# Score matmuls of an attention, split from four tiles of 32 by 128 into eight tiles of 32 by 64

## The chip, the cores and the metric

The kernel runs on one core of a Trainium2 chip. The metric is the device time of one execution in microseconds (us); lower is better. A core has engines that run at the same time and wait for one another by semaphores: TensorE (PE: matrix products, with a weight load before each one), VectorE (DVE), ScalarE (ACT), GpSimd (POOL), and SyncE (SP), which issues the DMAs here. Matrix products write into PSUM, which has eight banks of 128 partitions by 512 float32; everything else lies in SBUF.

## What is computed

Four layers follow one another on 16 images of 384 channels and 16 by 16 pixels, seen as 2 groups (`b`) of 2048 tokens. All is float32.

- Layer 0, attention with 12 heads of 32 channels over 2048 tokens: `out = alpha*v + beta*softmax(q k^T / sqrt(32)) v - gamma*mean(v)`, where `v` is the input itself and `q`, `k` are a product of the input with `qk_w`.
- Layer 1, a ConvNeXt block: a depthwise 7 by 7 convolution, a layer norm over channels, a product to 1536 channels, GELU, a global response norm, a product back to 384, and a residual.
- Layer 2: two Sobel filters, a product that fuses them, a layer norm, GELU, a residual.
- Layer 3: a 1 by 1, a 3 by 3 depthwise and a 1 by 1 convolution, a linear attention with 8 heads, and an MLP of 1536 channels.

## The kernel before

A block is 512 tokens of one group (`BLK`); there are eight, four for each group, and each is an SBUF tile of 128 partitions by 3 by 512.

**Attention.** `attention` runs over 6 units (`u`: a group `b` and a set `g` of four heads, which fill 128 partitions), in each over 4 query blocks (`n`), and in each over 16 key tiles of 128 tokens (`t`): 384 iterations. One iteration has two parts on TensorE.

- `scores(n, t)`: four matmuls, one for each head `h`. The keys are the weights (32 rows by 128 columns: the head's channels by 128 key tokens) and the queries stream through (32 rows by 512). The four stand in the four row groups of the array and run at once, and each fills a PSUM bank. Two heads share a tile `st` of two banks. The pool `pst` holds three such tiles, and an iteration takes two. ScalarE then forms the exponentials, two instructions of 128 by 1024 from `st` to `e`.
- `weighted(n, t, es)`, called one iteration later: four matmuls `av` with 128 rows by 32 columns, which stand in the four column groups. The denominators are not a product in each iteration: VectorE first adds up `ADDS[n]` (2 to 16) of the `e` tiles into `s`, and `weights` then sends the sums through TensorE against a column of ones (`dn`). `finish` inverts them and writes the block of layer 0.

At `t == SLOT` (5) a pair of projections `p` of the next block or unit is put in. A float32 matmul is carried out as two passes, so the profile shows two MATMUL and two LDWEIGHTS for each `pe.matmul`.

**What fills VectorE meanwhile.** After each iteration `attention` calls `fill(t, added)`. It asks `pace(t)` for the length of the iteration on TensorE (`pe`) and for the time that VectorE is needed in it (`dve`), and puts operations of layer 1 into what is left: for the first two blocks (`l1_0_0` and `l1_0_1`, the `leads`) the 7 by 7 convolution, 48 VectorE instructions for each of 3 channel groups after a first one on ScalarE (tile `y`), and after it the layer norm, as far as it comes. `pace` is a few constants; the first is 2.066 us for an iteration without `dn` and `p`.

**After attention.** A planner (`Plan.all`) orders all other work as the program is built, from estimated lengths, the tiles that are free and a rank of each task, starting from where `fill` left each task. PE, ACT and DVE then execute exactly that order (`InOrder`), so an instruction that waits holds all that is queued behind it on its engine. Layer 1 of a block has these steps by the names in the profile: taps `y<-l,vec,y`; sums `s_l` over channels and a product with ones `su_l` for the mean; `y<-su_l,y`; squares on ScalarE, their sum `s_l`, a product `sv_l` for the variance; a reciprocal, `y<-y,s_l`, an affine step on ScalarE; the first MLP product `ph_l` (36 matmuls of 128 by 128 by 512 for a block), GELU into `hid_l`, the response norm by way of `gx_l` and `pg_l`, and the second product `po_l`.

All matmuls, activations and vector operations are recorded through one helper (line 96), so the profile gives line 96 for all of them, and the names of the tiles tell them apart. `a<-b,c` reads: `a` is written from `b` and `c`.

Of the kernel before, what the change touches and what calls it, by code (L numbers as in the profile page):

```python
# [15 lines left out]
P = 128  # L16
# [7 lines left out]
HD = 32  # L24
# [32 lines left out]
TB = BLK // P  # L57
# [136 lines left out]
def pace(t):  # L194


    n, i = divmod(t - 1, NQC)
    adds = ADDS[n]
    pe, dve = 2.066, 2.275 if t and i % adds else 0.0
    at = i - adds - 1  # L200
    parts = sum(j * adds // 4 == at % adds for j in range(4)) if at >= 0 else 0
    if parts:
        pe += 0.22 * parts
    elif i == 1 and n > 0:
        pe += 0.87
    else:
        pe += 0.09
    if n > 0:
        dve += {2: 0.88, 3: 0.88, 4: 0.88, 5: 0.88, 6: 0.6, 7: 0.66}.get(i, 0.0)
    return pe, dve  # L210
# [187 lines left out]
def attention(tc, X, xt, L0, block, small, col, cols, ones, load_qk, banks, fill, bound):  # L398
# [4 lines left out]
    pe, act, dve = (InOrder(tc, e) for e in (nc.tensor, nc.scalar, nc.vector))  # L403
    units = [(b, g) for b in range(NB) for g in range(NC)]
    with ExitStack() as actx:
# [9 lines left out]
        def bank2(name):  # L415
            return pst.tile([P, 2, BLK], F32, tag="st", name=name)
# [38 lines left out]
        def unit(u, made, gm):  # L455

            b, g = units[u]
            q, keys, v = made["q"], made["k"], made["v"]
            adds = ADDS[u * NBLK : (u + 1) * NBLK]
            acc, sums = {}, {}  # L460

            def scores(n, t):
                es = []
                for i in range(2):
                    es.append(ep.tile([P, 2, BLK], F32, tag="e", name=f"e_{u}_{n}_{t}_{i}"))
                sts = [bank2(f"st_{u}_{n}_{t}_{i}") for i in range(2)]
                for h in range(4):
                    rows = slice(HD * h, HD * (h + 1))
                    pe.matmul(
                        sts[h // 2][:, h % 2, :],  # L470
                        keys[t // TB][rows, ts(t % TB, P)],
                        q[n][rows, :],
                        start=True,
                        stop=True,
                    )
                for i in range(2):
                    act.activation(es[i], sts[i], AF.Exp, scale=HD**-0.5)
                return es
# [56 lines left out]
            def finish(n, va, xg):  # L535
# [23 lines left out]
                for i, f in [*enumerate(todo), (8, check)]:  # L559
                    due.setdefault((k + 1) * NQC + 2 + i, []).append(f)  # L560

            return scores, weighted

        means = [channel_means(dve, op, X, cols, b, act if b else None) for b in range(NB)]
# [41 lines left out]
def conv_seq_kernel(  # L606
# [874 lines left out]
    if fast:  # L1481
# [5 lines left out]
        def fill(t, added=0.0):  # L1487
# [7 lines left out]
            if t % NQC == 9 and t > NQC:  # L1495
                u, i = divmod(t // NQC - 1, NBLK)
                plan.mark(("l0", u // NC, i, u % NC))
            length, work = pace(t)
            free = length + added - work - lag
            for task in (*leads, conv):  # L1500
# [157 lines left out]
```

## Time and profile before

| | |
|---|---|
| time, median of 3 executions | 2676.41 us (2674.85 to 2677.70) |
| span of the profiled execution | 2676.1 us |
| attention, first score matmul to the first `ph_l` | 20.7 to 1050.9 us |
| PE busy | 2645.0 us, 99% of the span |
| DVE busy | 2011.5 us, 75% |
| ACT busy | 1554.4 us, 58% |
| granted TensorE clock, mean | 0.996 |

The page states no time of the profiled execution apart from its span, which is the time from its first to its last instruction; it lies within the three times measured without the profiler and 0.3 us below their median, so sums are made against the span. "Busy" is the union of the intervals in which an engine has an instruction under way. For TensorE these intervals overlap, and their ends are modelled: 99% says that something was always under way, not that the array did useful work all the time. The starts of matmuls are what can be relied on.

### The profile page before, as it was taken

To read this page: it belongs to the slowest core of one execution; us is meant where nothing else is said; L and a number is where in the kernel's file an instruction comes from. 1 tells how busy PE (TensorE), PEld (TensorE's weight loads), DVE (VectorE), ACT (ScalarE), POOL (GpSimd) and SP (SyncE) were. 2 spreads that over 40 slices of the span, in tenths; PEclk is the share of its full clock that TensorE was granted. 3 is DMA by queue.
4 is the path that set the end of the run, shared out by engine and by line. 5 is a ranking of instruction groups with operands and counts; after the bars stand their busy time and mean duration, and the time that the engine had idled before them with its cause. 6 is when DMAs were issued, how large, how long until landed. Compare 5 with 4: busy or idle time off the path is not lost. (4 is left out here: it accounts for less than half of the span.)

```text
span 2676.1 us, 32807 instructions
## 1 busy us (share of the span) xinstructions
PE 2645.0 (99%) x12997; PEld 1061.0 (40%) x12997; DVE 2011.5 (75%) x2588; ACT 1554.4 (58%) x2314; POOL 7.4 (0%) x54
## 2 busy tenths in 40 slices
PE   9999999999999999899999999999999999999999
PEld 2223333233323323345444444444444444454443
DVE  6999999999999889999999999999652202722300
ACT  6787778878787888564565335357443542625201
POOL 0000000000000000000000000000000000000000
PEclk9999999999999999999999999999999999999999
DMA  3000000000000003000001001011001110000000
GB/s 150 5 13 1 9 9 5 13 1 5 13 1 1 1 13 113 18 1 0 1 1 48 24 12 33 27 36 36 24 24 36 48 36 24 0 1 1 12 17 20
DMA packets 29283, 55.69 MB, mean 21 GB/s; under 512 B 1728, under 2 KB 14400, under 8 KB 29120
## 3 DMA queue, kind: packets, MB, share of 16 engines
q1 hardware_dynamic: 29120, 53.51, 6.1%
q8 instruction: 104, 1.70, 0.3%
q14 instruction: 59, 0.48, 0.1%
HBM read 47.21 MB, written 6.29 MB: 20 GB/s over the span
## 5 line engine op out<-in xcount | busy, mean ns | idle before, releaser
L96 ACT ACTIVATE e<-st 128x1024 f32<-128x1024 f32 x768 | 742.4, 1024 | 89.2 <-PE st L96 81.3
L96 DVE SCALAR_TENSOR_TENSOR y<-l,vec,y 128x420 f32<-128x420 f32 (+8 forms) x1152 | 659.5, 633 | 5.0
L96 DVE TENSOR_TENSOR s<-s,e 128x1024 f32<-128x1024 f32 x444 | 512.9, 1212 | 11.8 <-ACT e L96 11.4
L96 PE MATMUL st<-q,k 32*128 32x512 f32 x3072 | 474.0, 641 | 4.0 <-ACT e L96 2.3
L96 PE MATMUL av<-e,v 128*32 128x512 f32 x3072 | 410.9, 606 | 4.3 <-ACT va L96 4.1
L96 PE MATMUL ph_l<-y,wa 128*128 128x512 f32 x576 | 261.4, 597 | 0.0
L96 PE MATMUL ph_l3c<-d_l3c,wa 128*128 128x512 f32 x576 | 258.4, 593 | 0.0
L96 PE MATMUL po_l<-hid_l,wb 128*128 128x512 f32 x576 | 255.8, 597 | 1.1 <-ACT hid_l L96 0.9
L96 PE MATMUL po_l3c<-hid_l3c,wb 128*128 128x512 f32 x576 | 256.6, 593 | 0.0
L96 PEld LDWEIGHTS st<-q,k 32*128 32x128 f32 x3072 | 145.9, 183 | 220.0 <-issue 132.5
L96 DVE TENSOR_TENSOR s<-e,e 128x1024 f32<-128x1024 f32 x162 | 190.9, 1220 | 47.5 <-ACT e L96 28.7
L96 ACT ACTIVATE hid_l<-ph_l,vec 128x512 f32<-128x512 f32 x96 | 65.8, 686 | 203.7 <-PE ph_l L96 203.6
L96 ACT ACTIVATE hid_l3c<-ph_l3c,vec 128x512 f32<-128x512 f32 x96 | 65.4, 685 | 203.0 <-PE ph_l3c L96 202.9
L96 PEld LDWEIGHTS av<-e,v 128*32 128x32 f32 x3072 | 60.6, 108 | 298.3 <-issue 273.4
L96 DVE SCALAR_TENSOR_TENSOR o_l3c<-po_l3c,vec,l 128x512 f32<-128x512 f32 x24 | 17.5, 746 | 209.6 <-PE po_l3c L96 208.8
L96 PEld LDWEIGHTS po_l<-hid_l,wb 128*128 128x128 f32 x576 | 109.6, 191 | 139.1 <-issue 128.1
L96 PEld LDWEIGHTS ph_l3c<-d_l3c,wa 128*128 128x128 f32 x576 | 108.8, 190 | 137.2 <-issue 133.2
L96 PEld LDWEIGHTS ph_l<-y,wa 128*128 128x128 f32 x576 | 109.1, 191 | 135.9 <-issue 124.9
L96 PEld LDWEIGHTS po_l3c<-hid_l3c,wb 128*128 128x128 f32 x576 | 109.0, 190 | 134.7 <-issue 132.8
L96 PE MATMUL p<-x,wqk_sb 128*128 128x512 f32 x288 | 133.2, 612 | 4.2 <-DMA x<-in_x_dram 4.1
L96 DVE SCALAR_TENSOR_TENSOR g_l3a<-h_l3a,dw,g_l3a 128x450 f32<-128x450 f32 (+1 forms) x192 | 119.0, 695 | 4.1 <-ACT g_l3a L96 4.1
L96 PEld LDWEIGHTS dn<-s,ones 128*32 128x32 f32 x2016 | 64.1, 110 | 125.4 <-issue 107.3
(150 smaller groups left out, 2442.0 us busy)
## 6 DMA issues: line engine op xcount, KB each, us to landing
wa<-in_w_dram SPq DMA_DIRECT2D x9, 768.0 KB, 4.5
wb<-in_w_dram SPq DMA_DIRECT2D x9, 768.0 KB, 5.1
wa<-in_mlp_w_dram SPq DMA_DIRECT2D x9, 768.0 KB, 4.5
wb<-in_mlp_w_dram SPq DMA_DIRECT2D x9, 768.0 KB, 4.6
v<-in_xt_dram SPq DMA_DIRECT2D x24, 256.0 KB, 2.7
out_dram<-o_l3c SPq DMA_DIRECT2D x24, 256.0 KB, 2.1
x<-in_x_dram SPq DMA_DIRECT2D x7, 768.0 KB, 10.8
qkv<-in_qkv_wT_dram SPq DMA_DIRECT2D x3, 576.0 KB, 10.8
```

What stands on the lines that cost most here:

```text
L96: self.last = self.tc.keep_in_program_order(make(*args, **kw))
```

## The change

Each score matmul is split by key tokens into two of 64 columns. The two halves of a head write the two halves of the partitions of the same bank, as `ts(j, 64)`. The eight matmuls of an iteration stand in four row groups by two column groups. What is computed, the tiles, their sizes and the pools stay as they are. In `pace` the first constant becomes 1.98.

```diff
@@ def pace(t):
-    pe, dve = 2.066, 2.275 if t and i % adds else 0.0
+    pe, dve = 1.98, 2.275 if t and i % adds else 0.0
@@ def scores(n, t):
                 for h in range(4):
-                    rows = slice(HD * h, HD * (h + 1))
-                    pe.matmul(
-                        sts[h // 2][:, h % 2, :],
-                        keys[t // TB][rows, ts(t % TB, P)],
-                        q[n][rows, :],
-                        start=True,
-                        stop=True,
-                    )
+                    rows = ts(h, HD)
+                    for j in range(2):
+                        pe.matmul(
+                            sts[h // 2][ts(j, 2 * HD), h % 2, :],
+                            keys[t // TB][rows, ts(2 * (t % TB) + j, 2 * HD)],
+                            q[n][rows, :],
+                            start=True,
+                            stop=True,
+                        )
```

## The prediction

> **What bounds the kernel now.** I read the page first, then busy time by stage, the score and `av` tiles, and stretches of the timeline.
>
> ```profile
> PE 2645.0 (99%) x12997; PEld 1061.0 (40%) x12997; DVE 2011.5 (75%) x2588; ACT 1554.4 (58%) x2314; POOL 7.4 (0%) x54
> ```
>
> Busy time by stage (us, then busy us and instructions for each engine, granted clock, DMA share, GB/s):
>
> ```profile
> 20.70:1050.90 1030.20, 1021.89 (x8423) 318.25 (x8422) 962.44 (x1013) 836.46 (x992) 0.00 (x0) 1.00 0.03 9
> 1050.90:1098.40 47.50, 39.80 (x102) 18.25 (x101) 42.56 (x65) 31.24 (x81) 0.00 (x0) 0.90 0.51 180
> 1098.40:1500.00 401.60, 397.05 (x1121) 180.89 (x1120) 391.53 (x630) 211.62 (x421) 1.94 (x14) 0.99 0.04 12
> ```
>
> TensorE sets the pace nearly everywhere, but VectorE is close behind: 962 of 1030 us in attention, 97% from 1098 to 1500. The one place where TensorE visibly starves is the hand-over at 1050 to 1098.
>
> An iteration with one part of `dn`, in the timeline of PE (start, length, group), and then one pair without `dn`:
>
> ```profile
> 704.39 1.14 PE L96 MATMUL st<-q,k 32*128 32x512 f32 x8
> 705.46 1.06 PE L96 MATMUL av<-e,v 128*32 128x512 f32 x8
> 706.35 0.40 PE L96 MATMUL dn<-s,ones 128*32 128x128 f32 x8
> 706.68 0.71 PE L96 MATMUL st<-q,k 32*128 32x512 f32 x4
> ```
>
> ```profile
> 733.16 1.14 PE L96 MATMUL st<-q,k 32*128 32x512 f32 x8
> 734.24 1.06 PE L96 MATMUL av<-e,v 128*32 128x512 f32 x8
> 735.23 1.31 PE L96 MATMUL st<-q,k 32*128 32x512 f32 x8
> 736.47 1.06 PE L96 MATMUL av<-e,v 128*32 128x512 f32 x8
> 737.47 0.71 PE L96 MATMUL st<-q,k 32*128 32x512 f32 x4
> ```
>
> The first takes 2.285 us. The second shows the two lengths that alternate wherever no `dn` is due: 2.067 and 2.238. In the longer one the second half of the scores starts 0.17 us late, because its bank is still being read by the exponential. So 226 iterations (with `dn`, `p` or both) are bound by TensorE alone, and 157 by TensorE and this loop in turn.
>
> The tile view (min/median/max ns) gives the parts of a score set:
>
> ```profile
> L96 PE MATMUL st<-q,k x3072: 587/692/1218, 20.7 to 1045.6; 32*128 32x512 f32 x192
> L96 PE MATMUL av<-e,v x3072: 592/617/1062, 24.8 to 1048.7; 128*32 128x512 f32 x192
> ```
>
> The smaller value is a second pass, the median a first one, which contains its weight load: 105 ns for 128 columns, 25 ns for 32. The single records of the set at 704.39 fit: first passes start at .393, .400, .406, .413 (6.7 ns per tile), second ones 533 ns later, and `av` follows at 705.462. Thus 1.071 us = 107 load + 427 + 427 stream + 20 until the fourth tile has started + 90 drain.
>
> The hand-over:
>
> ```profile
> 1050.90 20.87 PE L96 MATMUL ph_l<-y,wa 128*128 128x512 f32 x48
> 1071.61 2.06 PE L96 MATMUL pb<-sh,ca 128*128 128x1 f32 x18
> 1073.54 10.55 PE L96 MATMUL ph_l<-y,wa 128*128 128x512 f32 x24
> 1087.72 1.10 PE L96 MATMUL su_l<-s_l,ones 128*128 128x512 f32 x2 [3.64 <-DVE s_l L96]
> 1090.75 0.59 PE L96 MATMUL pg_l<-gs_l,ones 128*128 128x2 f32 x2 [1.94 <-DVE gs_l L96]
> 1093.46 2.04 PE L96 MATMUL sv_l<-s_l,ones 128*128 128x512 f32 x2 [2.12 <-DVE gmean_l L96]
> ```
>
> The first block's layer norm was finished inside attention, so `ph_l` starts at once; then TensorE waits for the second block's convolution and norm. Summed over gaps between starts, about 11.5 us are lost here, and some 8 us in all of the rest.
>
> **What the skill says.** The Trainium skill, "TensorE: Matmul & The Clock Gate", section "LDWEIGHTS", says that a load costs its columns divided by 1.2 GHz whatever its rows: 107 and 27 ns, which the 105 and 25 above confirm. Its Part 3 gives about 4 ns per further tile; the trace has 6.7, so I use 6.7. "TensorEngine Tiling (Array Packing)", section "Key Properties", says that a change of tiling mode drains the array; the records show 90 ns after a score set, 95 after `av`, and the change keeps both. The first page's Part 1 says that some 3.4 us of idleness halve the clock; the trace agrees (0.90 in the hand-over), and I price that at 2 us.
>
> **The change part by part.**
>
> *Score set.* The weights have 64 columns: load 107 to 53, -53 ns. Eight tiles instead of four: the last starts 47 ns after the first, not 20: +27. Streams unchanged: eight tiles take the 427 ns that four took. Issue: an iteration with two parts of `dn` would need 40 matmuls in some 2.45 us, 61 ns each; `pn_l3b` shows 57 ns each over 40 in a row, so this is not the bound. Drain: 90 kept; it was not seen to depend on width (95 ns after `p`, 128 wide, as after `av`, 32 wide). Net -26 ns. This form is not in the trace, so I bound it: 0, if loads or starts gain nothing, to -86, which the new pacing constant assumes.
>
> *Bank loop.* The first half of a set ends 40 ns earlier (load -53, two more tiles ahead +13) and the second half's normal start is 13 ns later, so the longer of the alternating lengths becomes 2.185: the pair falls from 4.304 to 2.040 + 2.185 = 4.225, 40 ns for each iteration.
>
> *Sum in attention:* 226 x 0.027 + 157 x 0.040 = 6.1 + 6.3 = -12.4 us (0 at the one end; 226 x 0.086 + 157 x 0.082 = -32 at the other).
>
> *Pacing constant.* `fill` takes every iteration to be 86 ns shorter, 33 us over 384, and puts that much less under attention. The changed instruction order shows it: 225 taps before the last `s` addition instead of 255 (30 x 0.63 = 19 us), and none of the first block's layer norm, which was inside. What was inside had its cost: table loads and a reciprocal in the exponentials' way (968.5 to 978.5) and smaller stalls lengthened iterations by 8.3 us, summed from 890 to 1040 over what each lasts beyond the same iteration of other units. These go: -8.3. The two products `su_l`, `sv_l` only move.
>
> *What is late next.* Now `ph_l` of the first block waits for the norm. Call T the end of the last `dn` (1050.9 before). VectorE in its new order, with durations from its timeline: r, va, l up to T+5.7; 14 taps of both blocks in turn at 0.51: 12.9; two `s_l`: 14.4; five taps of 0.63: 17.5; `y<-su_l` 1.7: 19.2; the weights' `fm`, `fw`, `ca` 7.2: 26.4; two `s_l`: 27.9; `sv_l` and its root until 30; five taps meanwhile: 31; reciprocal 3.35 and `y<-y,s_l` 1.75: 36.1; ScalarE's affine 0.8: `ph_l` starts at T+37. On TensorE only `su_l`, `pb`, `sv_l` are queued before it, since it executes in order. Nine groups of `ph_l` (23 us, +2 cold clock) to T+62. The second block has 39 taps left, 25.7 us, done at T+62; `su_l` at 63, `sv_l` at 70, root (behind `hid_l` and a table load on ScalarE) 73, reciprocal and scaling 78.4. `pg_l` at 79; `ph_l` of the second block to T+82; the scaled `hid_l` lets `po_l` start at T+83. Useful work in these 83 us: 30.7 `ph_l` + 2.6 `ph_l` + 4.3 `su_l`, `sv_l` + 2.1 `pb` + 0.3 = 40. Idle 43, against 11.5: **+31.6 us**.
>
> *Afterwards.* VectorE is then some 6 us further in its list than before at the same point, which may fill a part of the 8 us of later gaps: -2 (0 to -7). The end (2000 to 2676, DVE 25% busy) has room for everything. The order hardly differs there. DMAs are not moved.
>
> Sum: -12.4 - 8.3 + 31.6 - 2 = **+9 us**: 2676.1 + 9 = 2685 by the span, and as much by the median, which is 0.3 us away.
>
> **Rivals.** 0.2% (5.4 us) is about what a measurement of this kernel tells from no change.
>
> 1. *The score set gains what the constant assumes (faster).* If drain too shrinks with the tile and the eight starts cost nothing, an iteration without `dn` takes 1.98 us, attention gains 32 us and the sum is -11: 2665. Place: the step from the last score matmul to `av`. It decides from a mean gain of 56 ns per iteration, where 21.5 us pay for the hand-over. For it: 1.98 is near what a load of 53 less and a drain of 27 less would give. Against: the stagger of 6.7 ns is in every set of the trace, and the drain is the same for 32 and 128 columns.
> 2. *Half of that:* drain shrinks, stagger stays: about 53 ns per iteration and 66 in the loop, -22 us in attention, sum -1: 2675.
> 3. *No gain in the set:* eight tiles get in one another's way (two column tiles read the same 32 rows, issue doubles). Attention keeps its length, the smaller fill remains: +21, 2697. For it: the form is nowhere in the trace. Against: four `av` streams of 128 rows run at full rate.
>
> **How the numbers follow.** Forecast 0.48, rivals 0.28, 0.15, 0.09. Each has some 6 us either way from the hand-over (ScalarE's interleaving, cold clock) and the later gaps. The forecast's own range is 2677 to 2693: slower 3 in 4, else same. Rival 1: faster 5 in 6, else same; rival 2: mostly same; rival 3 slower. Slower 0.36+0.01+0.09 = 0.46; same 0.12+0.05+0.11 = 0.28; faster 0.23+0.03 = 0.26. A tenth lies below 2663 and about as much above 2695.
>
> **What would show it.** Score set to `av` 1.045 us instead of 1.071; iterations 2.26 with one part of `dn`, 2.04 and 2.185 in turn without; first passes some 53 ns longer than second ones; last `dn` near 1030; then a gap of over 30 us before `ph_l`, with only `su_l`, `pb`, `sv_l` in it; VectorE idle in attention by 15 to 25 us more. It is wrong if the set takes 0.99 or less (rival 1), if it stays at 1.07 or more (rival 3), or if `ph_l` follows the last `dn` at once.

## The result, and the profile after

The changed kernel takes 2708.03 us (median; 2707.28 to 2709.54) where the kernel before takes 2677.05 us on the same chip: a ratio of 1.0116, with a 95% interval of 1.0102 to 1.0130. It is slower by 1.2%, some 31 us. The forecast was 2685, with 2677 to 2693 as its own range and a tenth left above 2695, so the result lies well outside. The profiled execution has a span of 2705.3 us against 2676.1, so 29.2 us are to be found.

The page of the changed kernel, busy time by engine:

```profile
PE 2636.6 (97%) x16069; PEld 1028.2 (38%) x16069; DVE 2013.0 (74%) x2588; ACT 1570.9 (58%) x2326; POOL 7.4 (0%) x54
```

TensorE is under way for 8 us less than before although the span is 29 us longer. The busy time by stage shows where it stands still (same columns as before the change: stage and its length, PE, PEld, DVE, ACT, POOL, clock, DMA share, GB/s):

```profile
20.30:1031.80 1011.50, 1004.09 (x11491) 281.94 (x11490) 937.75 (x976) 828.48 (x982) 0.00 (x0) 1.00 0.03 10
1031.80:1116.10 84.30, 47.89 (x109) 22.34 (x108) 71.09 (x100) 40.74 (x91) 0.00 (x0) 0.76 0.29 102
1116.10:1530.00 413.90, 399.83 (x1124) 182.20 (x1123) 405.50 (x659) 220.87 (x430) 2.06 (x15) 0.99 0.04 12
```

Attention ends 19 us earlier. The hand-over, from the last `dn` to the first `po_l`, has grown to 84 us, in which TensorE works for 48 at a granted clock of 0.76. And in the 414 us after it TensorE is idle for 14, where the stretch of 402 us before had 4.6; VectorE is busy for 98% of it, against 97%.

Now the score set, the matmuls of one iteration that write `st`. The tile view of the changed kernel (min/median/max ns):

```profile
L96 PE MATMUL st<-q,k x6144: 587/588/639, 20.3 to 1026.5; 32*64 32x512 f32 x199
```

An iteration with one part of `dn` in its timeline of PE:

```profile
1014.54 1.12 PE L96 MATMUL st<-q,k 32*64 32x512 f32 x16
1015.59 1.06 PE L96 MATMUL av<-e,v 128*32 128x512 f32 x8
1016.48 0.40 PE L96 MATMUL dn<-s,ones 128*32 128x128 f32 x8
1016.81 1.11 PE L96 MATMUL st<-q,k 32*64 32x512 f32 x16
```

It lasts 2.27 us here and 2.258 in the median, 27 ns less than the 2.285 before; without `dn`, 2.040 and 2.204 alternate. Single records show first passes of 638 ns and second ones of 587. The 51 ns between them are the weight load of 64 columns; from the rule in the Trainium skill, "TensorE: Matmul & The Clock Gate", section "LDWEIGHTS" (columns divided by 1.2 GHz), 53 ns is the estimate for it, and it was 105 for 128 columns. The eight tiles of a set start 6.7 ns apart (47 ns from the first to the eighth, in the median), not the 4 of the same page's Part 3, and `av` follows a set after 1.044 us. So the set is 27 ns shorter where 26 were forecast, and the three rivals, which all lay here, have fallen. Rival 3 had the number that came nearest, 2697, but for a set that gains nothing.

The hand-over of the changed kernel:

```profile
1030.00 1.90 PE L96 MATMUL dn<-s,ones 128*32 128x128 f32 x16
1046.29 2.04 PE L96 MATMUL su_l<-s_l,ones 128*128 128x512 f32 x2 [14.39 <-DVE s_l L96]
1048.12 3.84 PE L96 MATMUL pb<-sh,ca 128*128 128x1 f32 x18
1059.26 2.08 PE L96 MATMUL sv_l<-s_l,ones 128*128 128x512 f32 x2 [7.29 <-DVE s_l L96]
1068.23 24.84 PE L96 MATMUL ph_l<-y,wa 128*128 128x512 f32 x54 [6.90 <-ACT y L96]
```

`ph_l` of the first block waits for its convolution and norm, which the smaller filling of attention has left over: it starts 36.3 us after the end of the last `dn`, and `po_l` 84 us after it.

Stage by stage, from the starts of matmuls (us):

| stage | before | after | difference | forecast |
|---|---|---|---|---|
| start to the first score matmul | 20.7 | 20.3 | -0.4 | |
| first score matmul to last `dn` | 1029.7 | 1011.0 | -18.7 | |
| the same, with 1.7 of `su_l`, `sv_l`, moved out, put back | | | -17.0 | -20.7 |
| last `dn` to first `po_l`, less the streams of what runs in it (32.4, 36.7) | 12.7 | 48.1 | +35.4 | +31.6 |
| first `po_l` to the end, with 2.6 of `ph_l`, done ahead, put back | 1580.6 | 1591.8 | +11.2 | -2 |
| sum | | | +29.2 | +9 |

The last line but one is what the forecast did not have.

A difference of 2 or 3 us within attention between two single executions says little: the changed kernel and two kernels below with the same instructions there (norm_first, after_ordsplit) take 1011.0 to 1012.9 us from the first score matmul to the last `dn`, and three kernels with the split and the old constant take 1018.9 to 1021.7.

### The profile page after: what moved, and what is told of

Same layout as the page of the kernel before. It is cut to its first block, busy times and chain, and to the rows that moved or that the text cites. A ratio compares the mean times of both kernels' runs of the same rounds, so it can differ in the third digit from the quotient of the medians.

```text
span 2705.3 us, 38965 instructions
## 1 busy us (share of the span) xinstructions
PE 2636.6 (97%) x16069; PEld 1028.2 (38%) x16069; DVE 2013.0 (74%) x2588; ACT 1570.9 (58%) x2326; POOL 7.4 (0%) x54
## 5 line engine op out<-in xcount | busy, mean ns | idle before, releaser
L96 DVE TENSOR_TENSOR s<-s,e 128x1024 f32<-128x1024 f32 x444 | 512.9, 1212 | 16.4 <-ACT e L96 16.0
L96 PE MATMUL st<-q,k 32*64 32x512 f32 x6144 | 459.7, 613 | 1.3 <-ACT e L96 1.1
L96 PEld LDWEIGHTS st<-q,k 32*64 32x64 f32 x6144 | 110.3, 129 | 217.3 <-PE st L96 114.0
## 6 DMA issues: line engine op xcount, KB each, us to landing
qkv<-in_qkv_wT_dram SPq DMA_DIRECT2D x3, 576.0 KB, 10.8
```

The source lines that it names most:

```text
L96: self.last = self.tc.keep_in_program_order(make(*args, **kw))
```

## The experiments

In all that follows, "gaps" are the times between the starts of two matmuls beyond what the first one streams (427 ns for 512 elements, less in proportion, but 60 ns at the least), where they are over 130 ns: for the hand-over from the last `dn` to 12 us after the first `po_l`, for the later part from there to the end. A smaller clock counts as a gap too.

| kernel | constant | later order | span | last `dn` | gaps, hand-over | gaps, later |
|---|---|---|---|---|---|---|
| before | 2.066 | planned for it | 2676.1 | 1050.4 | 11.5 | 8.2 |
| split_only | 2.066 | planned for it | 2668.1 | 1041.6 | 12.5 | 8.2 |
| const_only | 1.98 | planned for it | 2716.0 | 1041.7 | 46.6 | 19.3 |
| after | 1.98 | planned for it | 2705.3 | 1031.3 | 46.0 | 19.7 |
| norm_first | 1.98 | planned, another rank | 2701.6 | 1032.2 | 43.7 | 16.4 |
| split_202 | 2.02 | planned for it | 2699.8 | 1031.9 | 40.1 | 19.4 |
| split_204 | 2.04 | planned for it | 2691.9 | 1036.8 | 30.3 | 17.1 |
| split_2053 | 2.053 | planned for it | 2674.8 | 1042.2 | 19.4 | 7.0 |
| split_209 | 2.09 | planned for it | 2676.8 | 1040.4 | 8.9 | 19.8 |
| split_slack | 2.066 | planned, another slack | 2677.1 | 1041.0 | 12.5 | 18.7 |
| after_ordsplit | 1.98 | that of 2.066 | 2691.6 | 1032.5 | 43.4 | 8.2 |
| s209_ordsplit | 2.09 | that of 2.066 | 2665.0 | 1038.7 | 12.2 | 8.1 |
| s2066_ordafter | 2.066 | that of 1.98 | 2695.3 | 1039.5 | 29.8 | 19.5 |

Four theories were held against one another. A: the loss comes from the constant, which takes work out of attention. B: the split itself costs something, or its gain is lost. Then, for what is lost after the first `po_l`: C, it is the order that the planner arrives at; D, it is the VectorE work that is left over.

### The two halves of the change apart

split_only is the changed kernel with the old constant; const_only is the kernel before with the new one.

```diff
 # split_only, against the changed kernel
-    pe, dve = 1.98, 2.275 if t and i % adds else 0.0
+    pe, dve = 2.066, 2.275 if t and i % adds else 0.0
 # const_only, against the kernel before
-    pe, dve = 2.066, 2.275 if t and i % adds else 0.0
+    pe, dve = 1.98, 2.275 if t and i % adds else 0.0
```

> The score tiles are split, the pacing constant stays 2.066, so the order of all other work is that of the kernel before. Theory A (the loss is the constant's: it takes VectorE work out from under attention): attention is shorter by 10 to 12 us, the hand-over and all that follows look as before, 2664 to 2668 us. Theory B (the loss comes with the shorter attention: VectorE is the true bound up to 1560 us and only loses cover): attention gets shorter but later waits grow by as much, 2674 us or more.

> The score tiles stay 32 by 128, only the pacing constant becomes 1.98. Theory A: iterations stay 2.067 and 2.285, the wait before the first ph_l and the later waits of the changed kernel are there in full, so it is slower than the changed kernel by what the split gains: 2717 to 2721 us. Theory B: without the shorter attention there is less to wait for, 2690 to 2700 us.

split_only takes 2668.68 us, 0.9969 of before (0.9958 to 0.9979); const_only 2717.44, 1.0153 (1.0136 to 1.0170). By spans the split alone brings -8.0 us on the old constant and -10.7 on the new one; the constant alone costs +39.9 with the old tiles and +37.2 with the new. The two are nearly additive, so B has fallen and A stands. They should be: the planner goes by its estimates alone and doesn't see the split, and the traces show split_only carrying out the later work in the very order of the kernel before, and const_only in that of the changed kernel. split_only is faster than both kernels.

The hand-over of const_only in the timeline of PE:

```profile
1040.42 1.85 PE L96 MATMUL dn<-s,ones 128*32 128x128 f32 x16
1056.66 2.04 PE L96 MATMUL su_l<-s_l,ones 128*128 128x512 f32 x2 [14.39 <-DVE s_l L96]
1058.50 3.84 PE L96 MATMUL pb<-sh,ca 128*128 128x1 f32 x18
1069.63 2.07 PE L96 MATMUL sv_l<-s_l,ones 128*128 128x512 f32 x2 [7.30 <-DVE s_l L96]
1078.60 25.42 PE L96 MATMUL ph_l<-y,wa 128*128 128x512 f32 x54 [6.90 <-ACT y L96]
```

And that of split_only:

```profile
1040.26 1.90 PE L96 MATMUL dn<-s,ones 128*32 128x128 f32 x16
1042.09 20.87 PE L96 MATMUL ph_l<-y,wa 128*128 128x512 f32 x48
```

The waits of the changed kernel (14.39, 7.29, 6.90) stand in const_only to a hundredth, though not one score tile was touched; with the old constant and the new tiles `ph_l` follows the last `dn` at once.

split_only brings 7.9 us within attention where the split's part of the forecast was 12.4. split_slack and s2066_ordafter (below), with the same instructions inside attention, bring 8.5 and 10.8, so one execution gives this figure to some 3 us. Iterations bound by TensorE gain their 27 ns, but the alternating ones 30 ns in the mean of the changed kernel, not 40: 1.6 us less than forecast. Another 1.2 us of split_only lie in its first iteration of all, 6.32 us long instead of 5.13: it starts earlier, and `av` then waits 1.16 us in it for the transfer of `v`. The norm has no part in that.

### How much must be inside, and what goes first

```diff
 # split_204, split_2053, split_202: against the changed kernel
-    pe, dve = 1.98, 2.275 if t and i % adds else 0.0
+    pe, dve = 2.04, 2.275 if t and i % adds else 0.0      # 2.053, 2.02
 # norm_first: against the changed kernel
-    "l1": ((50.1, 89.5, 75.2, 4.0), (51.1, 16.8, 81.7, 28.5)),
+    "l1": ((-50.0, 89.5, 75.2, 4.0), (51.1, 16.8, 81.7, 28.5)),
```

norm_first leaves the filling as it is and only gives the first block the first place once attention is over.

> The split, with the constant at 2.040, the length that an iteration without dn really has in the changed kernel. 246 taps of the convolution lie before the last s addition (255 before, 225 in the changed kernel); of the first block's norm the reciprocal and the scaling come after attention. Theory A: the split gains its 10 to 12 us, a wait of 8 to 12 us before the first ph_l takes most of it back, less some 5 us of stalls in attention that go: 2666 to 2674 us. Rival (a constant that matches the real iteration is the best one): 2662 us or less, faster than with 2.066.

> The changed kernel with the rank of the first block's layer 1 at -50 instead of 50.1, so that the planner puts its last taps and its norm ahead of other work after attention (y<-y,s_l is the 40th VectorE instruction after the last s addition instead of the 45th, and it changes which work is taken later). If the wait before the first ph_l is what was lost (theory A), it shrinks from 36 us to about 25 to 30 and the time falls by as much, to some 2698 to 2703; if the later waits belong to VectorE being behind as a whole, they grow by as much and the time stays at 2708.

> The split with the constant at 2.053: 246 taps inside attention, as with 2.040, but the whole norm of the first block lies inside too (its last step is the 6th VectorE instruction ahead of the last s addition). If the wait before the first ph_l decides, it is gone or under 3 us, and the time is within 4 us of that with 2.066 (2667 to 2672). If the number of taps left over decides, it is near that with 2.040 (2686 to 2692).

> The split with the constant at 2.02: 238 taps inside, 143 of the first block's 144, and no step of its norm. Wait before the first ph_l of 22 to 30 us (36 with 1.98, 14 with 2.04), attention without the stalls of the norm (some 8 us shorter). If the wait before ph_l decides, 2692 to 2702 us; if the time follows the taps alone, between those of 2.04 and 1.98 in proportion, 2695 to 2698.

split_204 takes 2692.31 us, 1.0064 of before (1.0045 to 1.0083); norm_first 2701.60, 1.0094 (1.0077 to 1.0111); split_2053 2676.59, 0.9998 (0.9989 to 1.0007); split_202 2699.94, 1.0084 (1.0067 to 1.0101). Three things follow.

First, the gaps of the hand-over grow as the constant falls: 12.5 us at 2.066, then 19.4, 30.3, 40.1, and 46.0 at 1.98. At 2.053 two matmul records of `ph_l` run at once and the others wait 4.67 us for ScalarE's `y`; at 2.04 `ph_l` waits 13.05 us for it. Even 2.04, the length that the shortest iterations really have, is too small.

Second, it matters little what goes first once the work is late: norm_first takes 2.3 us from the 46.0 of gaps. Its time fell within the range expected, but not for the reason given: the wait from the last `dn` to the first `ph_l` shrank from 36.3 us to 34.7, not to 25 to 30, and 3.3 us of what went are later gaps, since its rank also changed the later order.

Third, the later gaps do not follow the constant: 7.0 and 8.2 us at 2.053 and 2.066, 16 to 20 at the others. Between 2.053 and 2.04 it is this jump of 10 us that adds to the 11 of the hand-over.

Two of the four missed what was expected. split_204 was to take 2666 to 2674 us: against split_only it has 17.8 us more gaps in the hand-over, where 8 to 12 were reckoned with, and 8.9 us more later, which were not in the sum at all. split_2053 was to take 2667 to 2672: it has 6.9 us more gaps in the hand-over.

### Order or work left over

split_209 puts still more inside than split_only (270 taps of the convolution before the last `s` instead of 255), so that less is left. split_slack puts the same inside as split_only and changes only how the planner chooses afterwards.

```diff
 # split_209: against the changed kernel
-    pe, dve = 1.98, 2.275 if t and i % adds else 0.0
+    pe, dve = 2.09, 2.275 if t and i % adds else 0.0
 # split_slack: against split_only
-SLACK = 0.196
+SLACK = 0.17
```

> The split with the constant at 2.09: 270 taps inside attention, 15 more than with 2.066, and the norm inside. Theory C (what was lost after the hand-over is the planner's order, which fits one starting state, and not VectorE work left over): attention and hand-over as with 2.066 or better, later waits longer, 2674 to 2684 us. Theory D (VectorE work left over decides): 9 us less of it is left, 2660 to 2668 us.

> The split with the constant 2.066 and the planner's SLACK at 0.17 instead of 0.196. The order inside attention is the same to the instruction, and so is the work left over; only the order after attention changes. Theory C: the time rises though nothing was moved, by 5 to 12 us to 2673 to 2681. Theory D: it stays at 2667 to 2671.

split_209 takes 2677.87 us (1.0004, 0.9995 to 1.0013) and split_slack 2677.31 (1.0002, 0.9994 to 1.0011), each some 9 us behind split_only. split_209 reaches `po_l` at the same time as split_only (1087.5 and 1087.6 us), with less left to do, and then loses as much as the changed kernel, which had more left: 19.8 and 19.7 us of gaps. D has fallen: the loss does not go with the amount. split_slack starts its first `po_l3c` (1522 us) 0.6 us before split_only and then falls behind by 9 us, half of it in one wait of `zb_l3b` on VectorE's `z_l3b`, of 4.40 us at 1590 us.

What such a wait is made of can be read in the changed kernel, in its timeline of PE, ACT and DVE, put in order of time, with other work left out:

```profile
1358.14 2.10 PE L96 MATMUL pv_l3b<-qkv,l 128*128 128x384 f32 x6
1359.05 0.21 ACT L96 ACTIVATE gx_l<-gx_l 128x24 f32<-128x24 f32 x1
1359.43 3.34 DVE L96 RECIPROCAL s_l3c<-s_l3c 128x512 f32<-128x512 f32 x1
1362.81 1.76 DVE L96 TENSOR_TENSOR d_l3c<-d_l3c,s_l3c 128x1536 f32<-128x1536 f32 x1
1364.48 0.17 DVE L96 TENSOR_REDUCE gs_l<-gx_l 128x2 f32<-128x24 f32 x1
1364.71 0.59 PE L96 MATMUL pg_l<-gs_l,ones 128*128 128x2 f32 x2 [4.48 <-DVE gs_l L96]
```

`gx_l` is there at 1359.26, and the sum of 0.17 us that TensorE needs from it runs at 1364.48: a reciprocal and a scaling of another layer stand ahead of it in VectorE's queue, and all of TensorE's queue stands behind `pg_l`. split_209, const_only and split_202 have the same wait with the same 4.64 us of gap, and another of 4.07 us before `pc_l3a`.

### The orders exchanged

One rival of C is left, D2: the state in which the later work starts is what costs, and no order helps. The last three kernels take the planner's choice away. The sequence of steps that it chose in split_only, or in the changed kernel, was written into the kernel as a list and carried out from another state. Steps that are already done inside attention are left out of the list; steps that are still open come first.

```diff
 # after_ordsplit: constant 1.98, list of 2.066
 # s209_ordsplit: constant 2.09, list of 2.066
 # s2066_ordafter: constant 2.066, list of 1.98
+    named = {t.name: t for t in tasks}
+    for a in "".join(ORDER) if fast else "":
+        assert plan.step(named[NAMES[a]]), NAMES[a]
     plan.all(tasks, SLACK)
...
+ORDER = (
...
```

> The changed kernel, with everything inside attention as it is (constant 1.98), but the later work in the order that was planned for the constant 2.066: first the 48 steps of the two leading blocks that the constant 2.066 had put inside, then that kernel's own order, step by step. Theory C (what is lost after the first po_l is the order that the planner arrives at, not the state that it starts from): TensorE's gaps after the first po_l fall from 19.7 us in the changed kernel to the 7 to 9 us of before and of split_only, although VectorE has as much work left as in the changed kernel; the hand-over still costs 40 us or more of gaps; the span is 2689 to 2698 (2705.3 less 8 to 16). Theory D2 (the state is what costs: VectorE is too late for any order): gaps after po_l stay at 15 to 20 us and the span is 2701 to 2710.

> The split scores with the constant 2.09, which puts 15 steps more inside than 2.066 does, and after it the order planned for 2.066, without those 15 steps. Theory C: the hand-over stays as in split_only or split_209 (9 to 13 us of gaps), the later gaps fall from the 19.8 us of split_209 to 7 to 9, and the span is 2664 to 2670 instead of 2676.8. Theory D2: 2675 to 2679, as split_209.

> The converse: the split scores with the constant 2.066, everything inside attention as in split_only, but the later work in the order that was planned for the constant 1.98 (the changed kernel's), without the 48 steps already done. Theory C: the later gaps rise from 8.2 us to 15 to 20, the hand-over stays short (9 to 14 us of gaps), and the span is 2675 to 2683 instead of 2668.1. Theory D2: the state is the good one, the later gaps stay at 7 to 10 and the span at 2665 to 2671.

after_ordsplit takes 2691.51 us, 1.0060 of before (1.0043 to 1.0077): by spans 13.7 us less than the changed kernel, with the same instructions inside attention. Its later gaps are 8.2 us instead of 19.7, which is 11.5 of it; 2.6 more are gaps of the hand-over. From the first `po_l` to the end it takes 1580.2 us, where before takes 1580.6 and split_only 1580.5. The same place as above, in its timeline:

```profile
1341.28 0.22 ACT L96 ACTIVATE gx_l<-gx_l 128x24 f32<-128x24 f32 x1
1342.86 0.17 DVE L96 TENSOR_REDUCE gs_l<-gx_l 128x2 f32<-128x24 f32 x1
1346.67 0.28 PE L96 MATMUL pg_l<-gs_l,ones 128*128 128x2 f32 x2
1352.05 3.34 DVE L96 RECIPROCAL s_l3c<-s_l3c 128x512 f32<-128x512 f32 x1
```

The sum now runs 9 us ahead of the reciprocal, and `pg_l` waits for nothing.

s209_ordsplit takes 2666.50 us, 0.9965 of before (0.9953 to 0.9978): the state of split_209, whose own order takes 11.8 us more by spans; its later gaps, 19.8 us against 8.1, are as much. With split_only, from which it can't be told apart, it is the fastest here.

s2066_ordafter takes 2697.69 us, 1.0086 (1.0070 to 1.0103). Its later gaps rise from 8.2 to 19.5 us, as C had it; its total missed the 2675 to 2683 expected, because the hand-over was expected to stay short and did not:

```profile
1038.21 1.89 PE L96 MATMUL dn<-s,ones 128*32 128x128 f32 x16
1055.64 3.97 PE L96 MATMUL pb<-sh,ca 128*128 128x1 f32 x18 [15.54 <-DMA ca<-in_cw1T_dram]
1059.48 26.16 PE L96 MATMUL ph_l<-y,wa 128*128 128x512 f32 x54
```

In the order of 1.98 `pb` stands ahead of `ph_l`. There its weights `ca` have the 16 us of the convolution to arrive; here the norm is done, and `ph_l`, which in split_only follows the last `dn` at once in the same state, is held behind a product that waits for a transfer. In split_only `pb` comes after 48 matmul records of `ph_l`, and does not wait. So in the hand-over an order can cost where it meets another state than its own; in the later part it costs the same in every state tried.

D2 has fallen with all three: both states run the later part with 8 us of gaps in the one order and with 19 to 20 in the other.

The traces say more than the three exchanges. Compared instruction by instruction, the thirteen kernels have only four later orders; kernels in one line of this table differ at most in the first 98 instructions of an engine after attention.

| later order | kernels | taps inside | gaps, later |
|---|---|---|---|
| I | before, split_only, split_2053, after_ordsplit, s209_ordsplit | 225 to 270 | 7.0 to 8.2 |
| II | const_only, after, split_202, split_209, s2066_ordafter | 225 to 270 | 19.3 to 19.8 |
| III | norm_first, split_204 | 225, 246 | 16.4, 17.1 |
| IV | split_slack | 255 | 18.7 |

The changed kernel and split_209, which leave the most and the least work over, were given the same order II by the planner and lose the same. In all thirteen the gaps go with the order and not with the amount that is left over.

## Why the prediction was wrong

**Score set: right.** 27 ns less against 26, by the load (51 ns left of 105) and the start of eight tiles at 6.7 ns, with the streams and the drain as they were. Rivals 1 to 3 needed a set of 0.98, 1.02 or 1.07 us; it is 1.044.

**Bank loop: right in kind, too large.** 30 ns for an iteration, not 40. The wait for the bank did not shrink as the working had it: in the longer iterations the second half starts 191 ns after the first one (median), 184 before. Without a wait it is 27 and 14, so the wait itself is 164 ns, after 170, where the working had 145. That is 1.6 us. The whole difference in attention, 3.7 us by the table, is not far above what single executions differ by.

**Stalls of the norm: about right.** The 162 iterations with one part of `dn` fall from 2525 to 2451 ns in the mean, of which 27 ns are the split; the other 47, times 162, are 7.6 us of stalls that have gone, against 8.3. The 18 iterations with a whole pair of projections grew by 68 ns in the mean instead of shrinking by 27: 1.7 us. In const_only they grew by 90, so this came with the constant. One sign that the prediction named was wrong: VectorE's idle time in attention grew by 6 us, not by 15 to 25, because attention became 18.7 us shorter while 24.7 us of VectorE's work left it.

**Hand-over: right, 3.8 us too small.** `ph_l` after 36.3 us (T+37), `po_l` after 84.2 (T+83), with only the three products between that were named. So the times are right to some 1 us; most of the 3.8 is that the forecast counted 40 us as useful work in it, where 36.7 are streamed. const_only shows the same waits without the split.

**"Afterwards": this is the step that failed.** It said -2 us, since VectorE would be further in its list, and that "the order hardly differs there". VectorE's place in its list is not what decides. The order does differ (II in place of I), and it costs 11 us more gaps whatever state it meets; carried out in split_only's order, the changed kernel loses none of it (8.2 us). The term was set at -2 us and measured +11.2. Of the 20 us between the forecast and the span, 13 are this term, 3.8 the hand-over and 3.3 attention with the start.

What stays open is why the planner arrives at order I with the constants 2.053 and 2.066, at order II with 1.98, 2.02 and 2.09, and at others with 2.04 or another rank or slack. What its estimated lengths miss at these places was not looked into, nor whether an order better than I exists.

## What to carry to other kernels

A constant in a planner's model moves work, and has to be priced by what it leaves for the place where that work is waited for: here 27 ns gained in an iteration were entered as 86, and what this took out of attention came back as 35 us in the hand-over. A greedy order that is built at compile time is part of the result: a small change of its start can give it another order, worth some 10 us here, which no list of instructions in the changed part shows. So a change that shifts a planner's start should be timed with the order held fixed as well, and the order compared where a short operation feeds the engine that sets the pace; if a good order is found, it can be kept as a list.

## What the runs showed of the hardware

Eight tiles of 32 by 64, of which two each read the same 32 rows, stream as fast as four of 32 by 128: the second pass of a tile starts 480 ns after its first one, where it was 533, which is 427 of stream in both and 53 of load instead of 106. Of what a narrower tile saves, this exposed load, the starts of four further tiles at 6.7 ns each take back half. The wait for the bank between the halves, 170 ns before and 164 after, hardly shrank with the set, which was not expected.
